# Layernorm's small arithmetic as a chain on GpSimd, and exponentials, masks and shift on two tiles at once, in a four-layer graph network

## The chip, the cores and the metric

The kernel runs on one core of a Trainium2 chip. The metric is the device time of one execution in microseconds, median of the runs. A profile comes from one further execution of the same program. Engines are called PE (TensorE, matrix products), DVE (VectorE), ACT (ScalarE), POOL (GpSimd) and SP (SyncE, which issues most DMAs here).

## The reference

32 batch elements, each with `x` of 512 nodes by 256 features and a 0/1 adjacency of 512 by 512, go through four attention layers. Every layer begins with the same step and ends with a residual sum:

```python
h = jnp.maximum(_layernorm(x, axis=-1), 0.0)   # (x - mean) / sqrt(var + 1e-5), then relu
x = x + layer(h, adj, ...)
```

- Layer 0: scores `(h att_W) h^T / sqrt(256)`, masked softmax, then twice `tanh(att (h W + b))`.
- Layer 1: scores `leaky_relu(src_i + dst_j)`, masked softmax, product with the values.
- Layer 2: `exp(-leaky_relu(s_i + d_j))` where there is an edge, divided by the row sum, then elu.
- Layer 3: scores with a bilinear term, leaky_relu, masked softmax, two more products, elu.

What the change touches is the mean and variance of layernorm in all four layers, and the exponential, mask and shift of the 512 by 512 scores in layers 1 to 3.

## The kernel before, in words

**Tiles.** 512 nodes are four tiles of 128 partitions. `x` of one batch element is a tile of 128 x 4 x 256 float32. The scores, transposed, are two tiles `e{l}_0` and `e{l}_1` of 128 x 2 x 512 float32 for each layer; `e(l, c)` is one 128 x 512 half of them. `codeT` holds the transposed adjacency in bfloat16.

**Who sets the order.** The program `graph(b, ...)` (L475) writes no instructions at once. Each `op(engine, cost, after, emit, tiles...)` notes a step: its engine, its cost as a pair of ns (how long it holds the engine, how long until its result can be used), the steps that it follows, and the tiles that it uses. `Plan.order` (L132) then plays all 32 elements with up to six in flight (`FLIGHT`, L244), gives each step a due time, and takes on each engine the ready step that is due first. `SLACK` (L68) stretches the costs for that: 1.03 for DVE (`V`) and ACT (`A`), 1.5 for POOL (`G`), and 0.8 us more for each DMA (`D`); 200 ns (`PASS`) go between steps. `Plan.best` (L91) tries several distances between the elements' due times and keeps the order that replays shortest. What comes out is one fixed order per engine, and each engine runs its list in that order; an instruction whose inputs are late holds up everything behind it on its engine.

**Layernorm**, `normed` (L552), in pairs of tiles, g = 0 and 1. For each tile `stats` (L556) runs `bn_stats` (L557, tile `st`: six numbers per row, among them the count-weighted statistics of the even and of the odd columns) and `bn_aggr` (L558, tile `mv`: mean and variance), both on DVE. For each pair DVE adds epsilon (`variance`, L561, tile `ve`), POOL takes the power -0.5 (`root`, L564, tile `rstd`), DVE forms minus mean times `rstd` (`offset`, L567, tile `off`). ACT then normalizes and clips each tile (`norm`, L571, tile `xn`). After it a copy splits `xn` into 16-bit planes (L576, on DVE, in layer 1 on ACT), SP issues a transposing DMA (L579, `planesT`), and ACT joins the planes to `hT` (L591), from which DVE makes sums `hs` (L664, L667) and PE the layer's products. Only in layer 0 of the first element are the tiles transposed by PE (L584).

**Scores of layers 1 and 2.** `leaky_exp_t` (L705) runs a leaky relu (L732) and an exponential (L735) for each of four tiles on ACT; `masked1` (L956) and `masked2` (L986) mask each tile on DVE. **Layer 3**: leaky relu (L1086, ACT), minus a row's maximum `crest` (L1089, DVE), exponential (L1092, ACT), each on four tiles. In every layer `attend` (L748) multiplies the tiles with the values on PE, tile by tile in the order c = 0 to 3 (L758).

**POOL** otherwise issues the weight loads at the start (L342) and the store of each finished element (L1154).

The pair of DVE's cost for `stats` and the costs of the power that the planner uses before the change:

```python
V_STATS, V_XN, V_TINY, V_TWO = (525.0, 610.0), (322.0, 407.0), (80.0, 165.0), (255.0, 340.0)
G_POW, G_STORE = (800.0, 850.0), (900.0, 900.0)
```

Of the kernel before, what the change touches and what calls it, by code (L numbers as in the profile page):

```python
# [11 lines left out]
F32 = mybir.dt.float32  # L12
# [3 lines left out]
AF = mybir.ActivationFunctionType  # L16
ALU = mybir.AluOpType
PSUM = bass.MemoryType.PSUM

P = 128  # L20
EPS = 1e-5
ALPHA = 0.2
NEG_INF = -(2.0**53)
TINY = 2.0**-100
# [11 lines left out]
    return t, t + 170.0  # L36


V_STATS, V_XN, V_TINY, V_TWO = (525.0, 610.0), (322.0, 407.0), (80.0, 165.0), (255.0, 340.0)
V_MASK, V_CODE, V_HALF, V_PSUM, V_ADD = (602.0, 683.0), (600.0, 690.0), (600.0, 690.0), (395.0, 484.0), (334.0, 425.0)  # L40
A_COPY, A_HALF, A_PRELU, A_EXP, A_TANH = (477.0, 597.0), (253.0, 373.0), (570.0, 693.0), (519.0, 640.0), (373.0, 474.0)
A_BIAS, A_PRELU2 = (570.0, 687.0), (629.0, 722.0)
G_POW, G_STORE = (800.0, 850.0), (900.0, 900.0)
V_SUM, V_BLOCK = (334.0, 425.0), (790.0, 880.0)
A_HALF_BIAS = (345.0, 460.0)
A_NORM, A_JOIN, V_SPLIT = (491.0, 590.0), (620.0, 767.0), (332.0, 422.0)
D_TURN = (1310.0, 2600.0)
# [159 lines left out]
def kernel(  # L207
# [48 lines left out]
    cols, pair, stat, turned = [P, HC, N], [P, NT, H], [P, NT], [P, NT, N]  # L256
# [8 lines left out]
        "code": (turned, BF16, "code"), "adj": (turned, I32, "adj"),  # L265
        "planes": ([P, 2, H], U16, "planes"), "planesT": ([P, 2 * HC, P], U16, "planesT"),
        "bank": ([P, 512], F32, "bank"), "v": (None, F32, "v"),
        "st": ([P, NT, 6], F32, None), "mv": ([P, NT, 2], F32, None), "sT": ([P, P], F32, "sT"),
        "ve": (stat, F32, None), "rstd": (stat, F32, None), "rs": (stat, F32, None), "off": (stat, F32, None),
# [155 lines left out]
    for n, dst, w, key in (("w0", w0_s, w0, "raw9"), ("att", att_s, att_w, "raw10")):  # L425
# [11 lines left out]
    a = [load(l1_sb, rows_of(l1_w), "raw0")]  # L437
    t = transposed(l1_sb, lambda: halves(l1_wide()), a, "raw0", "raw11")
# [36 lines left out]
    def graph(b, adj_before, x_before):  # L475


        T = Tiles(b)

        def op(engine, cost, after, emit, *keys, size=0, weights=()):  # L480
            return plan.op(engine, cost, after, emit, b, T.uses(keys) + W.uses(weights), size)

        def two(g):
            return slice(2 * g, 2 * g + 2)
# [67 lines left out]
        def normed(l, xs):  # L552
# [2 lines left out]

            def stats(t):  # L556
                nc.vector.bn_stats(T[f"st{l}"][:, t, :], T["x"][:, t, :])  # L557
                nc.vector.bn_aggr(T[f"mv{l}"][:, t, :], T[f"st{l}"][:, t, :])  # L558

            def variance(g):  # L560
                nc.vector.tensor_scalar(T[f"ve{l}"][:, two(g)], T[f"mv{l}"][:, two(g), 1], EPS, None, ALU.add)  # L561

            def root(g):
                nc.gpsimd.tensor_tensor(T[f"rstd{l}"][:, two(g)], T[f"ve{l}"][:, two(g)], mhalf[:, two(g)], ALU.pow)  # L564

            def offset(g):
                nc.vector.scalar_tensor_tensor(T[f"off{l}"][:, two(g)], T[f"mv{l}"][:, two(g), 0], -1.0,  # L567
                                               T[f"rstd{l}"][:, two(g)], ALU.mult, ALU.mult)

            def norm(t):  # L570
                nc.scalar.activation(T[f"xn{l}"][:, t, :], T["x"][:, t, :], AF.Relu,  # L571
# [23 lines left out]
            for g in range(NT // 2):  # L595
                a, d = (op("V", V_STATS, [xs[t]], partial(stats, t), "x", "slot") for t in (2 * g, 2 * g + 1))
                if b == l == 0:
                    for n in ("w0", "att"):
                        ready[n][0]["after"].append(d)
                a = op("V", V_TINY, [a, d], partial(variance, g))  # L600
                r = op("G", G_POW, [a], partial(root, g))
                r = op("V", V_TINY, [r], partial(offset, g))
                for t in (2 * g, 2 * g + 1):
                    flat, over = f"planes{l}_{t}", f"planesT{l}_{t}"
                    a = op("A", A_NORM, [r], partial(norm, t), "x", f"xn{l}")
                    if b == l == 0:
# [98 lines left out]
        def leaky_exp_t(l, vs, sign):  # L705
# [40 lines left out]
            return [op("A", A_EXP, [x], partial(exp, c), f"e{l}_{c // 2}") for c, x in enumerate(ls)]  # L746

        def attend(l, es, vs, use):  # L748

# [202 lines left out]
            xs += [op("V", V_MASK, [a], partial(add_z, g), "z0", "x")] * 2  # L952


        def masked1(c):
            nc.vector.scalar_tensor_tensor(e(1, c), T["codeT"][:, c, :], TINY, e(1, c), ALU.max, ALU.min)  # L956

        hs = normed(1, xs)
        right_after, right = block_sums("hs1", "hT1", lambda j, l: T["hT1"][:, j, half(l)], hs, left=False)
        vb = scored_values(1, right_after, right, l1_aug, ready["l1"])  # L960
        vs = [tuple(vb.values())] * NT
        es = leaky_exp_t(1, vs, 1.0)
        es = [op("V", V_MASK, [a], partial(masked1, c), "codeT", f"e1_{c // 2}") for c, a in enumerate(es)]
# [18 lines left out]
        vs = [tuple(vb.values())] * NT  # L982
        es = leaky_exp_t(2, vs, -1.0)

        def masked2(c):
            nc.vector.scalar_tensor_tensor(e(2, c), T["codeT"][:, c, :], 0.0, e(2, c), ALU.not_equal, ALU.mult)  # L986

        es = [op("V", V_MASK, [a], partial(masked2, c), "codeT", f"e2_{c // 2}") for c, a in enumerate(es)]

        def third(t, a, key):  # L990
            def sums():
# [87 lines left out]
        def shift():  # L1079
            return T["crest3"][:, 2:4, :].rearrange("p r n -> p (r n)").bitcast(F32)  # L1080
# [4 lines left out]
        def leaky3(c):  # L1085
            nc.scalar.activation(e(3, c), e(3, c), AF.Prelu, bias=zero, alpha=ALPHA)  # L1086

        def shifted(c):
            nc.vector.tensor_tensor(e(3, c), e(3, c), shift(), ALU.subtract)  # L1089

        def exp3(c):
            nc.scalar.activation(e(3, c), e(3, c), AF.Exp)  # L1092
# [108 lines left out]
```

## Time and profile before

| | before |
|---|---|
| median of 3 runs | 2353.38 us (2353.06 to 2353.42) |
| span of the profiled execution | 2353.1 us, 0.3 us under that median; no other time of that execution is given |
| PE busy | 2328.9 us |
| DVE busy | 2099.7 us |
| ACT busy | 1719.9 us |
| POOL busy | 254.2 us |
| granted TensorE clock, mean | 0.999 |
| DMA | 178.26 MB, mean 76 GB/s |

A line of the window view gives a stretch (us from the start of the span), its length, and then the busy us of PE, PEld (weight loads of PE), DVE, ACT and POOL with their numbers of instructions, the granted PE clock, the DMA engines' share and GB/s. A line of a group gives the line of the kernel, engine, operation, written and read tile, shapes and count, then total busy us, mean ns of one, and the idle time of the engine just before it with what ended it. A line of the timeline or the chain begins with the start and the length in us; neighbours that are alike are merged (`x2`). L12 is line 12 of the kernel before.

### The profile page before, as it was taken

How to read it: one execution, taken by the hardware profiler on the slowest of the kernel's cores; microseconds unless marked ns; L12 is line 12 of the kernel's file. 1: busy time of each engine (PE TensorE's matmuls, PEld its weight loads, DVE VectorE, ACT ScalarE, POOL GpSimd, SP SyncE). 2: the span in 40 equal slices, each digit the busy share in tenths (PEclk: the TensorE clock that was granted, in tenths of full speed). 3: DMA queues.
4: the chain of work that ended last, by engine and by line, in shares of the span. 5: the costliest groups of instructions: out<-in, count | busy, mean ns of one | idle time of the engine just before them, and what ended most of it. 6: DMA issues, size and time to landing. Idle time of an engine off the chain costs nothing.

```text
span 2353.1 us, 37623 instructions
## 1 busy us (share of the span) xinstructions
PE 2328.9 (99%) x12374; PEld 1992.0 (85%) x12374; DVE 2099.7 (89%) x6060; ACT 1719.9 (73%) x3421; POOL 254.2 (11%) x316
## 2 busy tenths in 40 slices
PE   8999999999999999999999999999999999999998
PEld 5789888888888888888898888888888888888887
DVE  8788899989889898898998889989898988987998
ACT  5677778767787677786777877677776778667874
POOL 3000101111011111011110010100101000010110
PEclk9999999999999999999999999999999999999999
DMA  7431233323333332333323334233343333321221
GB/s 192 106 78 28 57 79 79 88 66 83 72 75 84 78 83 66 70 88 90 82 58 74 80 85 90 54 82 70 88 91 68 86 68 73 86 54 33 55 49 42
DMA packets 429859, 178.26 MB, mean 76 GB/s; under 512 B 384128, under 2 KB 401664, under 8 KB 429664
## 3 DMA queue, kind: packets, MB, share of 16 engines
q1 hardware_dynamic: 424288, 157.51, 31.2%
q0 software_dynamic: 5232, 18.23, 2.4%
q8 instruction: 97, 1.59, 0.3%
q14 instruction: 98, 0.80, 0.1%
q10 hardware_dynamic: 144, 0.13, 0.0%
HBM read 67.64 MB, written 16.89 MB: 36 GB/s over the span
## 4 chain that ended last, share of the span: by engine, by line
PE 94%; DVE 4%; DMA 1%; ACT 1%; issue 0%; POOL 0%; DVEq 0%; ACTq 0%
PE bank_a L758 36%; PE bank_z L918 9%; PE bank_s3p L1040 5%; PE bank_o L936 4%; PE bank_q0p L874 4%; PE bank_f3p L783 4%; PE bank_w3p L809 4%; PE bank_v0p L809 4%; PE bank_f0p L783 4%; PE bank_s3q L1040 3%; PE bank_q0q L874 3%; PE bank_v1p L809 2%; PE bank_v3p L809 2%; PE bank_v2p L809 2%; PE bank_v3q L809 2%; PE bank_v1q L809 2%
## 5 line engine op out<-in xcount | busy, mean ns | idle before, releaser
L758 PE MATMUL bank_a<-v,e 128*128 128x258 f32 (+2 forms) x4096 | 1017.7, 381 | 0.9 <-DVE e L956 0.9
L758 PEld LDWEIGHTS bank_a<-v,e 128*128 128x128 f32 x4096 | 744.1, 190 | 108.9 <-issue 18.2
L591 ACT COPY hT<-planesT 128x512 uint16<-128x512 uint16 x508 | 377.8, 769 | 93.9 <-DMA planesT<-planes 93.2
L564 POOL TENSOR_TENSOR rstd<-ve,mhalf 128x2 f32<-128x2 f32 x256 | 216.0, 863 | 1732.3 <-DVE ve L561 1599.4
L571 ACT ACTIVATE xn<-x,off,rstd 128x256 f32<-128x256 f32 x512 | 278.0, 593 | 39.8 <-DVE off L567 38.9
L918 PE MATMUL bank_z<-e,y 128*128 128x512 f32 x512 | 240.8, 593 | 0.0
L557 DVE BATCH_NORM_STATS2 st<-x 128x6 f32<-128x256 f32 x512 | 210.5, 411 | 3.8 <-DMA x<-in_x_dram 3.8
L576 DVE COPY planes<-xn 128x512 uint16<-128x512 uint16 x380 | 156.4, 420 | 17.3 <-DMA planesT<-planes 10.2
L882 ACT ACTIVATE e<-e 128x512 f32<-128x512 f32 x124 | 77.8, 629 | 121.9 <-DVE e L893 61.8
L732 ACT ACTIVATE e<-row,v 128x512 f32<-128x512 f32 x224 | 156.6, 719 | 0.8 <-DMA row<-row 0.7
L735 ACT ACTIVATE e<-e 128x512 f32<-128x512 f32 x256 | 157.1, 630 | 0.0
L918 PEld LDWEIGHTS bank_z<-e,y 128*128 128x128 f32 x512 | 92.7, 190 | 64.9 <-issue 60.5
L695 ACT COPY v<-bank_v1p 128x258 f32<-128x258 f32 x128 | 47.7, 373 | 120.0 <-PE bank_v1p L809 119.3
L936 PE MATMUL bank_o<-w_sb,zT 128*128 128x256 f32 x512 | 118.5, 379 | 0.2 <-ACT zT L922 0.2
L1047 DVE SCALAR_TENSOR_TENSOR e<-bank_s3p,v,mask 128x256 f32<-128x256 f32 x256 | 111.0, 475 | 8.4 <-PE bank_a L758 4.4
L558 DVE BATCH_NORM_AGGREGATE mv<-st 128x2 f32<-128x6 f32 x512 | 93.2, 182 | 17.5
L936 PEld LDWEIGHTS bank_o<-w_sb,zT 128*128 128x128 f32 x512 | 95.8, 190 | 12.8 <-ACT zT L922 0.6
L664 DVE TENSOR_TENSOR hs<-hT,hs 128x256 f32<-128x256 f32 x254 | 105.1, 414 | 1.1
L667 DVE TENSOR_TENSOR hs<-hT 128x512 f32<-128x512 f32 x127 | 86.6, 682 | 14.5 <-ACT hT L591 14.3
L1086 ACT ACTIVATE e<-e,zero 128x512 f32<-128x512 f32 x128 | 88.2, 721 | 12.9 <-DVE crest L1064 11.4
L885 DVE TENSOR_TENSOR e<-bank_q0p,mask 128x512 f32<-128x512 f32 x124 | 84.5, 682 | 13.8 <-PE bank_q0p L874 12.3
L1089 DVE TENSOR_TENSOR e<-e,crest 128x512 f32<-128x512 f32 x128 | 85.9, 682 | 8.3 <-ACT crest L1083 8.1
(202 smaller groups left out, 4891.3 us busy)
## 6 DMA issues: line engine op xcount, KB each, us to landing
adj<-in_adj_dram SPq DMA_DIRECT2D x128, 256.0 KB
x<-in_x_dram SPq DMA_DIRECT2D x31, 512.0 KB
out_dram<-y POOLq DMA_DIRECT2D x31, 512.0 KB, 3.6
row<-row SPq DMA_DIRECT2D x56, 256.0 KB
planesT<-planes SPq DMA_TRANSPOSE x508
codeT<-code SPq DMA_TRANSPOSE x124
crest<-crest SPq DMA_TRANSPOSE x64
row<-sT SPq DMA_DIRECT2D x56, 2.0 KB
```

The costliest lines, as they stand in the source:

```text
L557: nc.vector.bn_stats(T[f"st{l}"][:, t, :], T["x"][:, t, :])
L564: nc.gpsimd.tensor_tensor(T[f"rstd{l}"][:, two(g)], T[f"ve{l}"][:, two(g)], mhalf[:, two(g)], ALU.pow)
L571: nc.scalar.activation(T[f"xn{l}"][:, t, :], T["x"][:, t, :], AF.Relu, bias=T[f"off{l}"][:, t : t + 1], scale=T[f"rstd{l}"][:, t : t + 1])
L591: nc.scalar.copy(bits[:, :, :, t * P : (t + 1) * P], T[f"planesT{l}_{t}"].rearrange("p (b c) n -> p b c n", b=2))
L735: nc.scalar.activation(e(l, c), e(l, c), AF.Exp, scale=sign)
L758: nc.tensor.matmul(T[key][:, : LEAD + H + 1 - lead], e(l, c)[:, t * P : (t + 1) * P], T[f"v{l}"][:, c, lead:], start=(c == 0), stop=(c == ...
L783: nc.tensor.matmul(p[:, : N // 2], w[:, x - 1, :], right(x), start=fresh, stop=True, skip_group_check=True)
L809: nc.tensor.matmul(p[:, j * k : (j + 1) * k], right(x)[:, j * P : (j + 1) * P], w[:, x - 1, :], start=fresh and j == 0, stop=True, skip_gr ...
L874: nc.tensor.matmul(p[:, j * N // 2 : (j + 1) * N // 2], right(x)[:, j * P : (j + 1) * P], left(x), start=fresh and j == 0, stop=True, skip ...
L918: nc.tensor.matmul(T[f"bank_z{k}"], T["y0"][:, c, k * P : (k + 1) * P], e(0, c), start=(c == 0), stop=(c == NT - 1))
L936: nc.tensor.matmul(T[key][:, j * H : (j + 1) * H], T["zT"][:, k, t * P : (t + 1) * P], w1_sb[:, k, :], start=(k == 0), stop=(k == HC - 1))
L1040: nc.tensor.matmul(p[:, j * N // 2 : (j + 1) * N // 2], left(x)[:, j * P : (j + 1) * P], right(x), start=fresh and j == 0, stop=True, skip ...
```

## The change

On DVE `stats` keeps only `bn_stats`. Aggregation, variance, power and offset of a pair of tiles become `moments`: ten instructions on POOL on 128 x 2 numbers, one step of the plan. They compute the variance from the two halves' statistics as (sum of both) / 256 + eps + (difference of the means)^2 / 4, and the offset as minus half the sum of the means times `rstd`. In layers 1 to 3 the exponential, in layers 1 and 2 the mask, and in layer 3 the leaky relu and the shift too take a whole `e{l}_{g}` of 128 x 2 x 512 in one instruction; the leaky relu of layers 1 and 2 stays by tile, and the attention's products follow the pair's step in place of the tile's. The planner's costs change with them.

```diff
-V_STATS, V_XN, V_TINY, V_TWO = (525.0, 610.0), ...
+V_STATS, V_XN, V_TINY, V_TWO = (340.0, 425.0), ...
-G_POW, G_STORE = (800.0, 850.0), (900.0, 900.0)
+G_CHAIN, G_STORE = (2200.0, 2250.0), (900.0, 900.0)
+V_SUM, V_BLOCK, V_FULL = (334.0, 425.0), (790.0, 880.0), (1140.0, 1225.0)
+A_EXP_TWO, A_PRELU_TWO = (960.0, 1070.0), (1050.0, 1160.0)
...
             def stats(t):
                 nc.vector.bn_stats(T[f"st{l}"][:, t, :], T["x"][:, t, :])
-                nc.vector.bn_aggr(T[f"mv{l}"][:, t, :], T[f"st{l}"][:, t, :])
-
-            def variance(g):
-                nc.vector.tensor_scalar(ve, mv[..., 1], EPS, None, ALU.add)
-            def root(g):
-                nc.gpsimd.tensor_tensor(rstd, ve, mhalf[:, two(g)], ALU.pow)
-            def offset(g):
-                nc.vector.scalar_tensor_tensor(off, mv[..., 0], -1.0, rstd, ALU.mult, ALU.mult)
+            def moments(g):
+                st = T[f"st{l}"][:, two(g), :]
+                gap, total, var, rstd, off = (T[f"{n}{l}"][:, two(g)] for n in ("gap", "sum", "var", "rstd", "off"))
+                gp = nc.gpsimd
+                gp.tensor_tensor(gap, st[:, :, 1], st[:, :, 4], ALU.subtract)
+                gp.tensor_tensor(var, st[:, :, 2], st[:, :, 5], ALU.add)
+                gp.tensor_tensor(gap, gap, gap, ALU.mult)
+                gp.tensor_scalar(var, var, 1.0 / H, EPS, ALU.mult, ALU.add)
+                gp.tensor_scalar(gap, gap, 0.25, None, ALU.mult)
+                gp.tensor_tensor(var, var, gap, ALU.add)
+                gp.tensor_tensor(rstd, var, mhalf[:, two(g)], ALU.pow)
+                gp.tensor_tensor(total, st[:, :, 1], st[:, :, 4], ALU.add)
+                gp.tensor_scalar(total, total, -0.5, None, ALU.mult)
+                gp.tensor_tensor(off, total, rstd, ALU.mult)
...
-                a = op("V", V_TINY, [a, d], partial(variance, g))
-                r = op("G", G_POW, [a], partial(root, g))
-                r = op("V", V_TINY, [r], partial(offset, g))
+                r = op("G", G_CHAIN, [a, d], partial(moments, g))
...
-            def exp(c):
-                nc.scalar.activation(e(l, c), e(l, c), AF.Exp, scale=sign)
+            def exp(g):
+                nc.scalar.activation(T[f"e{l}_{g}"], T[f"e{l}_{g}"], AF.Exp, scale=sign)
...
-        def masked1(c):
-            nc.vector.scalar_tensor_tensor(e(1, c), T["codeT"][:, c, :], TINY, e(1, c), ALU.max, ALU.min)
+        def masked1(g):
+            nc.vector.scalar_tensor_tensor(T[f"e1_{g}"], T["codeT"][:, two(g), :], TINY, T[f"e1_{g}"], ALU.max, ALU.min)
...
-        def shifted(c):
-            nc.vector.tensor_tensor(e(3, c), e(3, c), shift(), ALU.subtract)
+        def shifted(g):
+            nc.vector.tensor_tensor(T[f"e3_{g}"], T[f"e3_{g}"], shift().unsqueeze(1).to_broadcast([P, 2, N]), ALU.subtract)
...
```

`masked2`, `leaky3` and `exp3` are changed in the same way as these three.

More of the change, by code (lines that the diff above doesn't have):

```diff
@@ L36, in pe @@
     return t, t + 170.0
-V_STATS, V_XN, V_TINY, V_TWO = (525.0, 610.0), (322.0, 407.0), (80.0, 165.0), (255.0, 340.0)
+V_STATS, V_XN, V_TINY, V_TWO = (340.0, 425.0), (322.0, 407.0), (80.0, 165.0), (255.0, 340.0)
 V_MASK, V_CODE, V_HALF, V_PSUM, V_ADD = (602.0, 683.0), (600.0, 690.0), (600.0, 690.0), (395.0, 484.0), (334.0, 425.0)
@@ L42 @@
 A_BIAS, A_PRELU2 = (570.0, 687.0), (629.0, 722.0)
-G_POW, G_STORE = (800.0, 850.0), (900.0, 900.0)
-V_SUM, V_BLOCK = (334.0, 425.0), (790.0, 880.0)
+G_CHAIN, G_STORE = (2200.0, 2250.0), (900.0, 900.0)
+V_SUM, V_BLOCK, V_FULL = (334.0, 425.0), (790.0, 880.0), (1140.0, 1225.0)
+A_EXP_TWO, A_PRELU_TWO = (960.0, 1070.0), (1050.0, 1160.0)
 A_HALF_BIAS = (345.0, 460.0)
@@ L267 @@
         "bank": ([P, 512], F32, "bank"), "v": (None, F32, "v"),
-        "st": ([P, NT, 6], F32, None), "mv": ([P, NT, 2], F32, None), "sT": ([P, P], F32, "sT"),
-        "ve": (stat, F32, None), "rstd": (stat, F32, None), "rs": (stat, F32, None), "off": (stat, F32, None),
+        "st": ([P, NT, 6], F32, None), "sT": ([P, P], F32, "sT"),
+        "gap": (stat, F32, None), "sum": (stat, F32, None), "var": (stat, F32, None),
+        "rstd": (stat, F32, None), "rs": (stat, F32, None), "off": (stat, F32, None),
         "top": (stat, BF16, None),
@@ L557, in stats @@
                 nc.vector.bn_stats(T[f"st{l}"][:, t, :], T["x"][:, t, :])
-                nc.vector.bn_aggr(T[f"mv{l}"][:, t, :], T[f"st{l}"][:, t, :])
-            def variance(g):
-                nc.vector.tensor_scalar(T[f"ve{l}"][:, two(g)], T[f"mv{l}"][:, two(g), 1], EPS, None, ALU.add)
-            def root(g):
-                nc.gpsimd.tensor_tensor(T[f"rstd{l}"][:, two(g)], T[f"ve{l}"][:, two(g)], mhalf[:, two(g)], ALU.pow)
-            def offset(g):
-                nc.vector.scalar_tensor_tensor(T[f"off{l}"][:, two(g)], T[f"mv{l}"][:, two(g), 0], -1.0,
-                                               T[f"rstd{l}"][:, two(g)], ALU.mult, ALU.mult)
+            def moments(g):
[12 more added lines that the diff above has]
+                gp.tensor_tensor(off, total, rstd, ALU.mult)
             def norm(t):
@@ L745, in leaky_exp_t @@
             ls = [op("A", A_PRELU if turned else A_PRELU2, [a], partial(leaky, c), key, v, f"e{l}_{c // 2}") for c in range(NT)]
-            return [op("A", A_EXP, [x], partial(exp, c), f"e{l}_{c // 2}") for c, x in enumerate(ls)]
+            return [op("A", A_EXP_TWO, ls[two(g)], partial(exp, g), f"e{l}_{g}") for g in range(NT // 2)]
         def attend(l, es, vs, use):
@@ L962, in graph @@
         es = leaky_exp_t(1, vs, 1.0)
-        es = [op("V", V_MASK, [a], partial(masked1, c), "codeT", f"e1_{c // 2}") for c, a in enumerate(es)]
+        es = [op("V", V_FULL, [es[g]], partial(masked1, g), "codeT", f"e1_{g}") for g in (0, 1)]
+        es = [es[c // 2] for c in range(NT)]
         def second(t, a, key):
@@ L983, in graph, with masked2 @@
         es = leaky_exp_t(2, vs, -1.0)
-        def masked2(c):
-            nc.vector.scalar_tensor_tensor(e(2, c), T["codeT"][:, c, :], 0.0, e(2, c), ALU.not_equal, ALU.mult)
-        es = [op("V", V_MASK, [a], partial(masked2, c), "codeT", f"e2_{c // 2}") for c, a in enumerate(es)]
+        def masked2(g):
+            nc.vector.scalar_tensor_tensor(T[f"e2_{g}"], T["codeT"][:, two(g), :], 0.0, T[f"e2_{g}"], ALU.not_equal, ALU.mult)
+        es = [op("V", V_FULL, [es[g]], partial(masked2, g), "codeT", f"e2_{g}") for g in (0, 1)]
+        es = [es[c // 2] for c in range(NT)]
         def third(t, a, key):
@@ L1083, in leaky_row, with leaky3, exp3 @@
             nc.scalar.activation(shift(), T["crest3"][:, 0, :], AF.Prelu, bias=zero, alpha=ALPHA)
-        def leaky3(c):
-            nc.scalar.activation(e(3, c), e(3, c), AF.Prelu, bias=zero, alpha=ALPHA)
-        def shifted(c):
-            nc.vector.tensor_tensor(e(3, c), e(3, c), shift(), ALU.subtract)
-        def exp3(c):
-            nc.scalar.activation(e(3, c), e(3, c), AF.Exp)
+        def leaky3(g):
+            nc.scalar.activation(T[f"e3_{g}"], T[f"e3_{g}"], AF.Prelu, bias=zero, alpha=ALPHA)
+        def shifted(g):
+            nc.vector.tensor_tensor(T[f"e3_{g}"], T[f"e3_{g}"], shift().unsqueeze(1).to_broadcast([P, 2, N]), ALU.subtract)
+        def exp3(g):
+            nc.scalar.activation(T[f"e3_{g}"], T[f"e3_{g}"], AF.Exp)
         hi = [op("V", V_MASK, [ls[2 * g]], partial(higher, g), f"e3_{g}", "crest3") for g in range(2)]
@@ L1099, in graph @@
         row = op("A", A_PRELU2, [a], leaky_row, "crest3")
-        ls = [op("A", A_PRELU2, [a, hi[c // 2]], partial(leaky3, c), f"e3_{c // 2}") for c, a in enumerate(ls)]
-        ls = [op("V", V_MASK, [a, row], partial(shifted, c), "crest3", f"e3_{c // 2}") for c, a in enumerate(ls)]
-        es = [op("A", A_EXP, [a], partial(exp3, c), f"e3_{c // 2}") for c, a in enumerate(ls)]
+        ls = [op("A", A_PRELU_TWO, [ls[2 * g], hi[g]], partial(leaky3, g), f"e3_{g}") for g in (0, 1)]
+        ls = [op("V", V_FULL, [ls[g], row], partial(shifted, g), "crest3", f"e3_{g}") for g in (0, 1)]
+        es = [op("A", A_EXP_TWO, [ls[g]], partial(exp3, g), f"e3_{g}") for g in (0, 1)]
+        es = [es[c // 2] for c in range(NT)]
         def block_w(i, l):
```

## The prediction

> **What bounds the kernel now.** I read the page, then the busy time in windows, the chain that ended last, the groups of each engine, and timelines. TensorE (PE) is busy for all but 24.2 us of the span:
>
> ```profile
> span 2353.1 us, 37623 instructions
> ...
> PE 2328.9 (99%) x12374; PEld 1992.0 (85%) x12374; DVE 2099.7 (89%) x6060; ACT 1719.9 (73%) x3421; POOL 254.2 (11%) x316
> ```
>
> Nothing in this diff lowers PE's 2328.9 us, since no matmul is touched. In the chain that ended last the same `bank_o` stretch returns after 71.94 us, one batch element:
>
> ```profile
> 890.72 3.45 PE bank_o L936 x16
> ...
> 962.66 3.45 PE bank_o L936 x16
> ```
>
> In the window view (the stretch, its length, then busy us of PE, PEld, DVE, ACT, POOL) PE has no idle time in the middle; the loss is at the two ends:
>
> ```profile
> 0.00:40.00 40.00, 31.17 (x122) 20.80 (x123) 31.61 (x123) 20.52 (x39) 18.67 (x40) 1.00 0.84 221
> 40.00:80.00 40.00, 38.54 (x207) 31.85 (x206) 36.00 (x109) 23.61 (x46) 2.68 (x4) 1.00 0.55 119
> ...
> 1000.00:1040.00 40.00, 40.00 (x208) 33.15 (x207) 36.65 (x106) 31.30 (x63) 5.07 (x6) 1.00 0.45 102
> ...
> 2240.00:2280.00 40.00, 36.06 (x180) 30.81 (x179) 37.60 (x116) 34.96 (x74) 5.07 (x6) 0.96 0.20 43
> ```
>
> Of the 24.2 us, 8.8 lie before the first matmul, 1.5 between 40 and 80, some 6.5 behind the last matmul, and nearly all of the remaining 7.4 after 1880 (3.9 from 2240 to 2280). From 80 to 2120 PE is busy for 2038.4 of 2040 us. So the change can earn hardly more than the 9 us of waits inside the run; it can lose without such a limit, because every engine runs a fixed order.
>
> **What goes.** From DVE: 512 aggregations (L558, 93.2 us busy, 182 ns each), 256 variances (L561, 37.6 us), 256 offsets (L567, 37.3 us), 168 us in all. And six pairs of 128x512 operations per element (L956, L986, L1089) become 128x1024. One takes 683 ns, a 128x256 `hs` (L664) 414: 256 columns cost 269, 1024 columns 683 + 2 x 269 = 1221, so a pair saves 145 and 192 pairs 28 us. DVE falls from 2100 to some 1904 us. On ACT the exponentials (L735 630 ns, L1092 632) and L1086 (721) are joined: by L999 (469 for 256 columns, beside 630 for 512) a join saves 308 ns, 256 joins 79 us at most. Between 80 and 2120 all this lies beside a PE that never waits: **nothing is earned there**. What covers it is PE's 71.94 us per element; DVE needs 65.6 of them now.
>
> **What comes: a chain of ten on POOL, 256 times.** Today POOL does only the power. The trace has no small POOL arithmetic; its nearest rows (busy us, mean ns):
>
> ```profile
> L564 POOL TENSOR_TENSOR rstd<-ve,mhalf 128x2 f32<-128x2 f32 x256 | 216.0, 863 | 1732.3 <-DVE ve L561 1599.4 <-DVE off L567 53.6 <-ACT xn L571 25.8
> ...
> masks.py:199 POOL TENSOR_SCALAR_AFFINE_SELECT ident<-ident 128x128 f32<-128x128 f32 x1 | 0.3, 284 | 0.0
> ...
> masks.py:197 POOL MEMSET ident<- 128x128 f32 x1 | 0.2, 204 | 0.3 <-POOLq L1187 0.3
> ...
> L326 POOL MEMSET minus<- 128x1 f32 x1 | 0.1, 95 | 0.0
> ```
>
> The two memsets give 0.86 ns a column, so the select at 2 columns would take 284 - 126 x 0.86 = 176 ns. I take that for each of the nine (bounds: 95, the memset, and 863, the power), and 0.08 us for the hand-over to a dependent one (from `ve`'s end to the power's start in the timeline), six times: 9 x 0.176 + 6 x 0.08 + 0.69 (the power undisturbed) = 2.75 us. POOL also waits for DVE. The view of L564 gives the power's spread, and the timeline shows a slow pair:
>
> ```profile
> L564 POOL TENSOR_TENSOR rstd<-ve,mhalf x256: 678/706/2346, 7.2 to 2279.2; 128x2 f32<-128x2 f32 x128
> ```
>
> ```profile
> 506.14 0.68 DVE L1009 SCALAR_TENSOR_TENSOR x<-y,x 128x512 f32<-128x512 f32 x1
> 506.24 2.33 POOL L564 TENSOR_TENSOR rstd<-ve,mhalf 128x2 f32<-128x2 f32 x2 [9.16 <-DVE ve L561]
> 506.74 0.68 DVE L519 TENSOR_SCALAR code<-adj 128x1024 bf16<-128x1024 int32 x1
> ```
>
> Two powers take 2.33 us beside these DVE operations, 1.38 in the quiet head. The mean is 863 - 690 = 173 ns over the undisturbed power; ten such waits are 1.7. **One chain: 4.4 us** (bounds: 9 x 0.095 + 0.69 = 1.5, and ten powers, 8.6).
>
> The Trainium skill ("SBUF — State Buffer", Who interferes with whom) says that a DVE instruction with two SBUF inputs and a GpSimd instruction that reads SBUF exclude each other, whoever starts second waiting for the other's whole instruction. The slow pair agrees with it; the mean row shows that a wait is usually much shorter than a whole DVE operation. By the strict form, ten full waits of 0.68 us, the chain would be an estimated 2.75 + 6.8 = 9.6 us; by the row it is 4.4.
>
> What does the chain replace? Not the 0.69 us of a power: `ve` and `off` stand in DVE's queue. At 613.69 two `ve` start, the powers end at 615.27, and the `off` run at 615.98 and 616.73, behind masks and sums. Over all 256 in the trace (k-th `ve` to k-th `off`) it is 2.9 us in the median and 3.4 in the mean from the start of the one to the end of the other, and the aggregation adds 0.2 ahead. So `xn` comes some 0.8 us later. In the 68 cases of 256 where two powers are asked for within 2 us, the second chain queues behind the first and its `xn` comes about 5 us later.
>
> The order knows of it: it is built with 2.25 x 1.5 = 3.4 us per chain, so my chain is 1.0 us late on it, a second one 2.0. Behind `xn` on ACT stand the evacuations of PE's banks. What takes up the delay is ACT's idle 27% and the 0.8 us that the order adds to each DMA, one of which (the transposition) follows every `xn`. Cost in the middle: from 0 to the rival's price; I take 1.6 us, a doubling of the 1.6 us that slip there now. On POOL itself stores and weight loads queue behind the chain; a store only frees its slot, 40 us before anyone asks (POOL idles 42.5 us ahead of one).
>
> **Head.** Tiles 0 and 1 have their statistics at about 5.4 us when no aggregation stands between. With DVE nearly idle the chain is 2.75 us: 8.2, as now (8.1). The second chain ends at 10.9, where `off` ended at 9.3: 1.6 us later, less what PE can multiply of `bank_v` meanwhile. I take +1.0 (0 to 1.6; weight loads behind more chains could add the 1.5 us again that PE waits between 40 and 80).
>
> **Tail.** From 2250 to 2272 PE idles 3.3 us and DVE is busy 20.8 of 22. There DVE loses 7 aggregations, 4 `ve`, 4 `off` and four joins: 1.3 + 0.6 + 0.6 + 0.6 = 3.1 us. Against it stands the later `xn`, 0.8 to 5 us, in the layers that nothing else covers. I take -1.5 (from -3.3 to +4).
>
> **Sum:** 1.6 + 1.0 - 1.5 = +1.1 us on the span of 2353.1, 2354.2; the median of the runs stands 0.3 above that span: **2354.5 us**. Ends without a rival: 2353.4 - 3.3 (tail) - 3.5 (the other waits after 1880) = 2346.6, and 2353.4 + 1.6 (middle) + 3.1 (head and loads) + 4 (tail) = 2362.1.
>
> **Rivals.** *Within a few us* (the sum above): 2354.5, 2349 to 2358.
>
> *POOL becomes late, slower.* Place: `xn` at the head of ACT's queue. DVE operations that read two SBUF tensors follow one another (414 to 683 ns, after the join 1221), so a chain of dependent reads may meet one each time: with half a 0.55 us operation per step, 2.75 + 10 x 0.27 = 5.4 us, 2.0 late on the order, 1.2 after the DMA's 0.8. If one chain in 25 passes that to PE (a guess; ACT idles for 27%), 10 x 1.2 = 12 us: **2366**. It decides from a chain of 4.2 us up (3.4 + 0.8); at 71.94 / 8 = 9.0 us POOL itself would be the bound. For it: mean over median in the power's row. Against: the old path through DVE was nearly as long.
>
> *DVE's relief fills the tail, faster.* If the chain is 3.4 us or less, `xn` comes no later than now, and of the 7.4 us of waits near the end and the 1.5 in the head some 7 go: **2346**. For it: DVE at 20.8 of 22 us where PE waits. Against: ACT is at 20.5 of 22 there too.
>
> *It does not relieve DVE*, since POOL's reads hold DVE up: DVE has 6 us per element to spare, so this too is within a few us, without the tail's gain: 2356.
>
> **Chances.** About 0.2% (4.7 us) is what a measurement of this kernel can tell from no change: under 2348.7 is faster, over 2358.1 slower. Within a few us, with the last rival: 0.44; POOL late: 0.36; tail filled: 0.20. The range takes in the faster rival and most of the slower one: 2346 to 2370.
>
> **What would show it.** The first POOL step takes about 176 ns and a chain about 4.4 us from first start to `off`; DVE falls to some 1904 us, ACT to 1640 to 1700; the period stays at 71.94; PE idles nearer 10 than 8.8 us at the start. It is wrong if the period grows, if ACT shows long waits for POOL ahead of `xn`, or if PE's waits after 1880 vanish or double.

## The result, and the profile after

| | before | after |
|---|---|---|
| median of 4 runs each | 2353.22 us (2352.96 to 2353.42) | 2364.28 us (2363.70 to 2365.25) |
| ratio to before | | 1.0046 (95% interval 1.0032 to 1.0060) |
| span of the profiled execution | 2353.1 us | 2363.0 us |

The change costs 11.1 us, where 1.1 were forecast. That is inside the range, and on the side and near the price of the rival "POOL becomes late" (2366); the likeliest case, 2349 to 2358, did not come. A later profiled execution of the kernel before, where span and time are both given, took 2352.58 us with a span of 2350.8: 1.8 us lie around the span, as after the change (2364.85 and 2363.0). The profiled execution of before was so some 1.5 us slower than its usual run, and the two profiles differ by 9.9 us.

The head of the page after (span, then busy us, share and instructions of each engine):

```profile
span 2363.0 us, 38600 instructions
...
PE 2331.4 (99%) x12374; PEld 1989.5 (84%) x12374; DVE 1980.0 (84%) x4844; ACT 1702.3 (72%) x3165; POOL 851.2 (36%) x2620
```

DVE lost 120 us and ACT 18; POOL gained 597. PE idles 31.6 us in place of 24.2. The window view after, with the columns of the prediction's:

```profile
0.00:20.00 20.00, 8.79 (x26) 5.71 (x27) 11.95 (x39) 5.42 (x10) 12.15 (x57) 1.00 0.77 243
20.00:40.00 20.00, 19.04 (x80) 12.44 (x79) 13.68 (x36) 11.94 (x23) 17.97 (x46) 1.00 0.70 161
...
80.00:2120.00 2040.00, 2036.25 (x10804) 1740.77 (x10803) 1718.75 (x4201) 1490.83 (x2776) 732.75 (x2262) 1.00 0.33 76
2120.00:2200.00 80.00, 80.00 (x439) 68.78 (x437) 58.91 (x139) 56.49 (x107) 19.25 (x66) 1.00 0.17 39
2200.00:2363.00 163.00, 148.94 (x834) 129.95 (x832) 144.03 (x345) 112.47 (x203) 46.28 (x124) 0.99 0.21 47
```

The number of matmuls has to be read beside the busy time. The same stretch of the middle before:

```profile
80.00:2120.00 2040.00, 2038.36 (x10835) 1747.69 (x10835) 1825.59 (x5259) 1507.13 (x3003) 212.27 (x250) 1.00 0.34 76
```

It has 10835 matmuls, and after the change 10804; at 2040 / 10835 = 0.188 us each, 31 fewer are 5.8 us. PE's busy time shows only 2.1 us of it. A matmul's record outlasts the start of the next one (379 ns for 256 columns in `bank_o`, where the next starts after 216), so a start that is up to 0.16 us late leaves no gap, and the late matmul itself is recorded some 0.1 us longer. So the loss is counted from start to start here: for every matmul the time to the next one's start, less the undisturbed pace of its shape. The choice of that pace shifts the middle of all kernels together by up to 1 us, so the differences between kernels count, and a value near 0 means no loss.

| us lost by PE | before the first matmul | 0-80 | 80-300 | 300-2120 | 2120-2200 | 2200-end | span |
|---|---|---|---|---|---|---|---|
| before | 8.8 | 5.5 | -0.1 | 1.9 | 2.5 | 8.8 | 2353.1 |
| after | 10.5 | 6.9 | 0.5 | 7.8 | -0.1 | 12.2 | 2363.0 |

After less before: 3.1 us up to 80, 0.6 and 5.9 in the middle, -2.6 and +3.4 near the end, -0.6 behind the last matmul, together 9.9 with rounding. There are two questions: the start, and the middle.

**The start**, in the timeline after:

```profile
6.85 0.20 POOL L565 TENSOR_TENSOR gap<-st 128x2 f32<-128x2 f32 x1 [5.30 <-DVE st L559]
...
8.29 0.72 POOL L571 TENSOR_TENSOR rstd<-var,mhalf 128x2 f32<-128x2 f32 x1
...
9.56 0.20 POOL L574 TENSOR_TENSOR off<-sum,rstd 128x2 f32<-128x2 f32 x1
...
9.80 1.09 ACT L577 ACTIVATE xn<-x,off,rstd 128x256 f32<-128x256 f32 x2 [7.14 <-POOL off L574]
...
10.45 1.18 PE L590 MATMUL bank_n<-ident,xn 128*128 128x128 f32 x4 [10.45 <-ACT xn L577]
```

An undisturbed chain takes 6.85 to 9.76, 2.9 us, and PE waits for it. Statistics begin 0.7 us later than before (5.35, were 4.64), since `x` landed later in this execution. The second chain ends at 12.92 and the weight loads on POOL begin at 18.7, where it was 12.6.

**The middle**, in the chain that ended last: the share by engine on the page, then stretches from its list.

```profile
PE 81%; POOL 7%; DVE 5%; ACT 4%; issue 2%; DMA 1%; POOLq 0%; SPq 0%; ACTq 0%; DVEq 0%
```

```profile
977.60 1.73 PE bank_o L940 x8
...
1024.29 0.48 POOL off L574
...
1029.37 1.04 POOL off L574
...
1030.94 0.58 ACT xn L577
1031.52 0.26 ACT v L699
...
1034.67 0.27 ACT v L699
...
1034.98 1.57 PE bank_a L762 x6
...
1050.02 1.73 PE bank_o L940 x8
```

Before, PE had 94% and POOL 0% of this chain. Now it runs through two POOL chains back to back, then on ACT through `xn` and the copies `v` out of PE's banks, to PE; and the same `bank_o` stretch returns after 72.42 us in place of 71.94. (Single elements take 69 to 78 us, so the loss is read from the table and not from one period.) The longest wait of PE that the view names between 300 and 2120 is 0.7 us. That looks like the slower rival. The experiments say how far it is.

### The profile page after: what moved, and what is told of

Same layout as the page of the kernel before. It is cut to its first block, busy times and chain, and to the rows that moved or that the text cites. A ratio compares the mean times of both kernels' runs of the same rounds, so it can differ in the third digit from the quotient of the medians.

```text
span 2363.0 us, 38600 instructions
## 1 busy us (share of the span) xinstructions
PE 2331.4 (99%) x12374; PEld 1989.5 (84%) x12374; DVE 1980.0 (84%) x4844; ACT 1702.3 (72%) x3165; POOL 851.2 (36%) x2620
## 4 chain that ended last, share of the span: by engine, by line
PE 81%; POOL 7%; DVE 5%; ACT 4%; issue 2%; DMA 1%; POOLq 0%; SPq 0%; ACTq 0%; DVEq 0%
PE bank_a L762 30%; PE bank_z L922 9%; PE bank_o L940 5%; PE bank_s3p L1046 4%; PE bank_q0p L878 4%; PE bank_f3p L787 4%; PE bank_f0p L787 4%; PE bank_v0p L813 3%; PE bank_w3p L813 3%; PE bank_s3q L1046 3%; PE bank_q0q L878 2%; PE bank_v3p L813 2%; POOL rstd L571 2%; PE bank_v1p L813 2%; PE bank_v2p L813 2%
## 5 line engine op out<-in xcount | busy, mean ns | idle before, releaser
L762 PE MATMUL bank_a<-v,e 128*128 128x258 f32 (+2 forms) x4096 | 1040.3, 381 | 5.7 <-ACT v L699 1.5
L565 POOL TENSOR_TENSOR gap<-st 128x2 f32<-128x2 f32 x256 | 77.5, 303 | 792.1 <-DVE st L559 737.2
L1161 POOL DMA_DIRECT2D out_dram<-y x31 | 25.8, 831 | 584.3 <-DVE y L1144 551.8
L571 POOL TENSOR_TENSOR rstd<-var,mhalf 128x2 f32<-128x2 f32 x256 | 209.2, 817 | 20.1
L559 DVE BATCH_NORM_STATS2 st<-x 128x6 f32<-128x256 f32 x512 | 191.4, 415 | 6.0 <-DMA x<-in_x_dram 5.6
L699 ACT COPY v<-bank_v3p 128x258 f32<-128x258 f32 x128 | 48.0, 375 | 128.8 <-PE bank_v3p L813 128.8
L739 ACT ACTIVATE e<-e 128x1024 f32<-128x1024 f32 x128 | 135.9, 1062 | 0.9
L960 DVE SCALAR_TENSOR_TENSOR e<-codeT,e 128x1024 f32<-128x1024 bf16 x64 | 78.3, 1223 | 38.5 <-ACT e L739 37.2
L703 DVE TENSOR_TENSOR v<-v,bank_v2q 128x258 f32<-128x258 f32 x96 | 40.4, 421 | 77.8 <-PE bank_v2q L813 73.4
L886 ACT ACTIVATE e<-e 128x512 f32<-128x512 f32 x124 | 78.9, 640 | 25.0 <-DVE e L897 23.3
```

Of the source, the lines that this page charges most:

```text
L571: gp.tensor_tensor(rstd, var, mhalf[:, two(g)], ALU.pow)
L762: nc.tensor.matmul(T[key][:, : LEAD + H + 1 - lead], e(l, c)[:, t * P : (t + 1) * P], T[f"v{l}"][:, c, lead:], start=(c == 0), stop=(c == ...
```

## The experiments

The expectations speak of theories by letters. In short, A: the chain's length on POOL reaches PE through `xn`. B: the two-tile steps hand their results on later. C: neither matters, the planner found a less lucky order. D: it is DVE's two-tile steps together with the chain. A ratio stands against the kernel before, run on the same chip (2353.2 to 2354.1 us). "Before" and "after" name the kernels before and after the change.

### The parts alone

The chain alone, with exponentials, masks and shift by tile as before:

```diff
-            def exp(g):
-                nc.scalar.activation(T[f"e{l}_{g}"], T[f"e{l}_{g}"], AF.Exp, scale=sign)
+            def exp(c):
+                nc.scalar.activation(e(l, c), e(l, c), AF.Exp, scale=sign)
...
```

`masked1`, `masked2`, `leaky3`, `shifted` and `exp3` go back in the same way.

> The chain of ten on GpSimd alone, with its planner costs; exponentials, masks and shift by tile as before. Theory A (the chain makes the normalized tile late, at the start and a little in every element): most of the 11 us of the whole change is here, 2360 to 2364 us, first matmul near 10.4 us, small PE waits in every element. Theory B (the joined two-tile steps make the attention start later): 2354 to 2356 us, only the start is late. Theory C (neither costs anything by itself, the new order is just a worse one): any value, no relation to the other runs.

Measured: 2360.02 us, 1.0031 (1.0019 to 1.0042). The size is as theory A had it, the place is not: from 300 to 2120 this kernel loses 0.5 us, less than before (1.9), with a period of 71.94 us in most elements. Its loss is at the start, in 80 to 300 (4.9 us) and near the end (11.2).

The two-tile steps alone, with the old layernorm:

```diff
-                r = op("G", G_CHAIN, [a, d], partial(moments, g))
+                a = op("V", V_TINY, [a, d], partial(variance, g))
+                r = op("G", G_POW, [a], partial(root, g))
+                r = op("V", V_TINY, [r], partial(offset, g))
```

> The two-tile exponentials, masks and shift alone; layernorm on DVE with the power on GpSimd as before. Theory A: 2350 to 2354 us, since only DVE and ACT are relieved, period 71.94 us per element, first matmul at 8.8 us. Theory B: 2358 to 2362 us with waits in every element. Theory C: any value.

Measured: 2357.03 us, 1.0015 (1.0007 to 1.0024), between the two expectations. It earns nothing and loses a little, again not in the middle (1.4 us there).

### The planner's cost

The kernel before, with nothing changed but what the planner believes of the power:

```diff
-G_POW, G_STORE = (800.0, 850.0), (900.0, 900.0)
+G_POW, G_STORE = (2200.0, 2250.0), (900.0, 900.0)
```

> The kernel before, instruction for instruction, but planned as if the power on GpSimd took 2.2 us (the cost of the chain), so that only the order differs. Theory A: the order plans the normalized tile 2 us later than it comes, which costs a little at the start, 2353 to 2356 us, and no waits in the middle. Theory C (the order is what costs): 2360 us or more.

Measured: 2355.56 us, 1.0009 (1.0000 to 1.0018). The first matmul starts at 11.5 us in this order, and the time hardly moves.

The kernel after, with the planner told the measured chain:

```diff
-G_CHAIN, G_STORE = (2200.0, 2250.0), (900.0, 900.0)
+G_CHAIN, G_STORE = (3000.0, 3700.0), (900.0, 900.0)
```

> The changed kernel, planned with the chain's measured length (3.0 us on the engine, 3.7 to its result) in place of 2.2. Theory A in the form that the order is taken by surprise: the waits in the middle go, 2357 to 2360 us, the late start stays. Theory A in the form that the delay costs by itself: 2363 to 2366 us, as the change. Theory B: no difference from the change, 2364 us.

Measured: 2363.70 us, 1.0043 (1.0030 to 1.0057): nothing gained. Yet POOL is off the path: 0% of the chain, and the wait view (us in total, times, longest) has almost no ACT waiting for it. Its lines from 300 to 2120:

```profile
ACT xn L577 <- POOL off L574: 11.7, 2, 8.2
...
PEld bank_z L922 <- DVE v L703: 5.3, 22, 0.2
...
PEld bank_v2p L813 <- ACT v L699: 4.6, 22, 0.2
```

Here two hand-offs of 0.2 us repeat in 22 elements, 5.3 + 4.6 = 9.9 us of waits on PE's weight loads, and PE's loss by starts in this stretch is 7.3. All but two of 24 elements take 72.32 to 72.34 us, 0.39 over 71.94. **The same loss as after, with another last step**: an evacuation of `v`, and no POOL before it.

### The order kept

The kernel before with its order as it stands; only what the steps issue differs. Aggregation, variance and offset issue nothing, and the ten instructions stand in the power's place:

```diff
-                nc.gpsimd.tensor_tensor(T[f"rstd{l}"][:, two(g)], T[f"ve{l}"][:, two(g)], mhalf[:, two(g)], ALU.pow)
+                moments(g)
```

> The order of the kernel before is kept step for step; only, the ten GpSimd instructions run where the power ran, and the aggregation, variance and offset are left out of DVE's list. Nothing else is joined. Theory A (the chain's length is what costs): the order expects a result after 0.85 us and gets it after 3.5, so ACT waits ahead of the normalized tile and PE behind it in every element: 2365 to 2385 us. Theory C (the new order costs, not the chain): 2352 to 2355 us.

Measured: 2374.60 us, 1.0091 (1.0076 to 1.0107), 20.5 us over before. The theory that only the order differs falls. The chain that ended last has POOL in it, by its shares:

```profile
PE 85%; POOL 6%; DVE 4%; ACT 3%; issue 1%; DMA 1%; SPq 0%; DVEq 0%; POOLq 0%; ACTq 0%
```

It loses 10.2 us from 300 to 2120, 8.2 more than before. The delay from a pair's statistics to `off` is not longer in the median: 3.9 us, where before it was 4.8. It has a floor (none is under 2.97, where 47 of before's were), but the floor is not what PE meets. The order is the same, so each matmul can be set beside its counterpart before. In the middle PE falls further behind eight times, by 0.85 to 2.1 us, and each time the chain of waits leads back over `xn` to a pair that had not been hurried before (3.2 to 5.2 us, here 5.9 to 9.2), and whose chain had queued behind another. Five of the eight are alike, one in every fourth element. The first of them, from the timelines of POOL, ACT and PE:

```profile
549.20 0.20 POOL L573 TENSOR_TENSOR off<-sum,rstd 128x2 f32<-128x2 f32 x1
549.35 0.20 POOL L564 TENSOR_TENSOR gap<-st 128x2 f32<-128x2 f32 x1
...
553.27 0.20 POOL L573 TENSOR_TENSOR off<-sum,rstd 128x2 f32<-128x2 f32 x1
...
553.50 0.60 ACT L585 ACTIVATE xn<-x,off,rstd 128x256 f32<-128x256 f32 x1 [0.78 <-POOL off L573]
554.00 0.46 ACT L807 ACTIVATE fa<-bank_f3p,l_u 128x256 f32<-128x256 f32 x1
...
554.51 0.70 PE L797 MATMUL bank_f3p<-hs,m 128*128 128x256 f32 x2 [0.17 <-ACT fa L807]
```

The same second `off` and the same matmuls before, from the timelines of DVE and PE:

```profile
545.29 0.15 DVE L567 SCALAR_TENSOR_TENSOR off<-mv,rstd 128x2 f32<-128x2 f32 x1
...
547.38 0.60 PE L783 MATMUL bank_f3p<-hs,m 128*128 128x256 f32 x2
```

There the second `off` ended 5.24 us after the pair's statistics, here 7.07. Before, it stood 1.9 us ahead of the matmuls; here they wait for it. Of the 18.4 us between the two profiles 6.8 come up to 300 us, 8.2 in the middle and 3.4 behind it.

Ten more dependent instructions on POOL, which add zero to `off`:

```diff
+                spare = gap
+                gp.tensor_tensor(spare, total, rstd, ALU.mult)
+                for i in range(7):
+                    gp.tensor_tensor(spare, spare, rstd, ALU.mult)
+                gp.tensor_tensor(spare, spare, spare, ALU.subtract)
+                gp.tensor_tensor(off, off, spare, ALU.add)
```

> The changed kernel with ten more dependent small instructions behind each chain, which add zero; the planner is told nothing of them. Theory A: a chain of 6.5 to 7.5 us in place of 3.7, ACT waits for GpSimd grow from 160 us to 500 or more, PE waits in every element, 2385 to 2420 us. Theory C: 2364 us.

Measured: 3042.30 us, 1.2925 (1.2907 to 1.2942), far over the 2385 to 2420 of theory A. The mean chain grew from 3.7 to 6.5 us, and the time by 678 us. Lines of its page (busy, and the chain's share) and of its waits:

```profile
PE 2545.8 (84%) x12374; PEld 2107.3 (69%) x12374; DVE 1990.2 (65%) x4844; ACT 1697.8 (56%) x3165; POOL 1375.4 (45%) x5180
...
POOL 43%; PE 32%; issue 10%; DVE 9%; ACT 5%; DMA 0%; POOLq 0%; ACTq 0%; SPq 0%; DVEq 0%
```

```profile
ACT xn L583 <- POOL off L580: 865.3, 243, 9.1
```

POOL is busy for 45% only: it is latency that costs, not POOL's throughput. A second chain waits for the first, and from statistics to `off` the median is 12.7 us. PE's busy time rose by 214 us although its matmuls are the same, for the granted clock fell to 0.924 in the mean. What the last 2.8 us of a chain cost is out of all proportion to the first 2.9.

### The start

The kernel after, with layer 0 of the first six elements on the old path through DVE:

```diff
+            early = l == 0 and b < FLIGHT
...
-                r = op("G", G_CHAIN, [a, d], partial(moments, g))
+                if early:
+                    a = op("V", V_TINY, [a, d], partial(variance, g))
+                    r = op("G", G_POW, [a], partial(root, g))
+                    r = op("V", V_TINY, [r], partial(offset, g))
+                else:
+                    r = op("G", G_CHAIN, [a, d], partial(moments, g))
```

> The changed kernel, but layer 0 of the first six elements has its aggregation, variance and offset on DVE and only the power on GpSimd, as before. If the start of the changed kernel (first 80 us, 3.1 us of the 9.9 between the two profiles) is the chain's doing, the first matmul is back near 8.8 us and the time falls by 2 to 4 us, to 2360 to 2362; if the late start is only swallowed further on, 2364.

Measured: 2361.45 us, 1.0031 (1.0019 to 1.0043), 2.8 under after in the medians. Its first window:

```profile
0.00:20.00 20.00, 10.90 (x37) 7.24 (x38) 13.09 (x54) 6.89 (x12) 7.38 (x24) 1.00 0.96 288
```

PE has 37 matmuls there, after had 26; the first starts at 8.6 us. The middle loses 7.7 as in after. So the start is the chain's price, about 3 us in this kernel, and is apart from the middle.

### Which join

The chain with ACT's steps joined and DVE's by tile (the cut shows the difference from the chain alone; `leaky3` and `exp3` likewise):

```diff
-            def exp(c):
-                nc.scalar.activation(e(l, c), e(l, c), AF.Exp, scale=sign)
+            def exp(g):
+                nc.scalar.activation(T[f"e{l}_{g}"], T[f"e{l}_{g}"], AF.Exp, scale=sign)
```

> The changed kernel with ACT's exponentials and layer 3's leaky relu joined, but DVE's masks and shift by tile as before. Theory A' (the 1.22 us DVE instructions hold the chain up, which makes the waits of the middle): GpSimd's small steps fall back to the means of the chain alone, waits in the middle go, 2359 to 2361 us. Theory B (the joins delay attention): half of the middle's waits stay, 2361 to 2363.

Measured: 2352.72 us, 0.9996 (0.9988 to 1.0005), the time of before and under both expectations. The middle loses nothing:

```profile
80.00:2120.00 2040.00, 2039.92 (x10849) 1749.41 (x10848) 1743.57 (x4385) 1489.87 (x2787) 721.19 (x2266) 1.00 0.34 76
```

14 more matmuls than before, 45 more than after. In the mean the chains are no shorter (3.64 us, after 3.70), so it is not the typical chain that DVE's joined operations make dear. The share of chains that follow another back to back fell, from 157 of 255 in after to 85. That alone does not decide either: it is 80 to 103 in the chain alone, in the kept order, with DVE's steps joined and in the two kernels with the planner's corrected cost, and two of these five have the loss. The two together are counted below.

The chain with DVE's steps joined and ACT's by tile:

```diff
-            def masked1(c):
-                nc.vector.scalar_tensor_tensor(e(1, c), T["codeT"][:, c, :], TINY, e(1, c), ALU.max, ALU.min)
+            def masked1(g):
+                nc.vector.scalar_tensor_tensor(T[f"e1_{g}"], T["codeT"][:, two(g), :], TINY, T[f"e1_{g}"], ALU.max, ALU.min)
...
```

`masked2` and `shifted` are joined in the same way.

> The changed kernel with DVE's masks and shift joined and the chain on GpSimd, but ACT's steps by tile: the corner that is missing. Theory D (the chain and DVE's joined steps do not go together): waits in the middle of 5 us or more, 2362 to 2368 us. If ACT's join has a part in it: 2357 to 2360 and no waits in the middle.

Measured: 2356.50 us, 1.0013 (1.0004 to 1.0021). The theory that the chain and DVE's two-tile steps are enough to make the loss falls: the middle loses -0.5 us, that is, nothing. And in this kernel the waits of ACT for POOL are longer in total than in any other but the doubled chain. The waits of the kernel with ACT joined, then those of this one:

```profile
ACT xn L577 <- POOL off L574: 184.6, 100, 6.1
```

```profile
ACT xn L577 <- POOL off L574: 280.1, 118, 5.8
```

In after they are 160.0 us in 139 times. 280 us of waits came with no loss in the middle, and the 24 us (in the whole span) of the planner's corrected cost with 7 us: **a wait on ACT ahead of `xn` is no sign of a loss**; only whether PE is reached counts.

ACT's steps joined, without the chain:

```diff
-            return [op("A", A_EXP, [x], partial(exp, c), f"e{l}_{c // 2}") for c, x in enumerate(ls)]
+            return [op("A", A_EXP_TWO, ls[two(g)], partial(exp, g), f"e{l}_{g}") for g in range(NT // 2)]
```

> ACT's exponentials and layer 3's leaky relu joined, nothing else: layernorm with the power on GpSimd, masks and shift by tile, as before. If ACT's join is a gain of its own (it made the chain's 2360.0 into 2352.7), 2346 to 2350 us. If it only made up for what the chain costs, 2352 to 2355.

Measured: 2360.84 us (2357.91 to 2364.15), 1.0033 (1.0021 to 1.0046): both expectations wrong. With no chain at all the profiled execution, the slowest of the five, loses 12.5 us from 300 to 2120, the most of any but the doubled chain, and the longest wait of PE there is another hand-off again (us in total, times, longest):

```profile
PE bank_f3p L784 <- ACT fa L794: 4.2, 5, 1.7
```

### The best version

The chain with ACT's steps joined, and layer 0 of the first six elements on the old path, as in the run on the start:

```diff
+            early = l == 0 and b < FLIGHT
...
+                    r = op("V", V_TINY, [r], partial(offset, g))
```

> Chain on GpSimd and ACT's steps joined, DVE's by tile (2352.7 us before), and layer 0 of the first six elements on DVE as before. If the start's loss is the chain's there too (first matmul at 9.4, 4.4 us of waits in the first 20), 2349 to 2351 us, faster than both kernels; if another order swallows it, 2352 to 2354.

Measured: 2351.29 us, 0.9991 (0.9982 to 1.0000), 1.4 under the same without the old start, and the lowest of all. It is 2 us under before, less than the 0.2% that can be told from no change.

The same kernel with ACT joined, with the planner's cost corrected:

```diff
-G_CHAIN, G_STORE = (2200.0, 2250.0), (900.0, 900.0)
+G_CHAIN, G_STORE = (3000.0, 3700.0), (900.0, 900.0)
```

> Chain on GpSimd and ACT's steps joined, DVE's by tile, but planned with the chain's measured length (3.0 us on the engine, 3.7 to its result): the same instructions in another order. If 2352.7 us is the work's and not one order's luck, 2351 to 2355 us; Theory C (orders differ by luck): 2356 to 2362.

Measured: 2353.98 us, 1.0001 (0.9992 to 1.0010). Three pairs of kernels differ by the planner's cost alone; measured against before, they lie 2.0, 0.9 and 2.1 us apart. The 11 us of the change are more than that.

### What is shown, and what stays open

| steps | us against before | PE's loss 300-2120 |
|---|---|---|
| chain | +6.5 | 0.5 |
| ACT joined | +7.6 | 12.5 |
| ACT and DVE joined | +3.5 | 1.4 |
| chain, ACT joined | -1.4 (other cost +0.7) | -0.6 (-0.6) |
| chain, DVE joined | +3.3 | -0.5 |
| chain, ACT and DVE joined (the change) | +11.1 (other cost +10.1) | 7.8 (7.3) |

(The numbers in brackets are of the same instructions, planned with the corrected cost.)

*What reaches PE in after.* Between 300 and 2120 us 47 matmuls start over 50 ns late, 9.1 us in all. Followed back in the trace, 42 of them, with 7.9 us, lead over ACT (`v` or `w`, then `xn`) to 23 of the 201 chains there. All 23 are long, 4.8 to 5.7 us where the mean is 3.7: in each, one or two steps of 0.2 us last 0.8 to 1.3 us beside a joined shift or mask of DVE. And 21 of them had first waited 1.6 to 2.6 us for the chain ahead. The stretch at 1029.37 shown above is one of these. So PE meets the two delays almost only where they fall together. Counted from 300 to 2120, chains that followed another within 0.3 us and then took over 4.5 us:

| kernel | such chains | PE's loss 300-2120 |
|---|---|---|
| the change | 25 | 7.8 |
| the change, old start | 25 | 7.7 |
| chain alone | 1 | 0.5 |
| chain, ACT joined (and with the other cost) | 0 (0) | -0.6 (-0.6) |
| chain, DVE joined | 0 | -0.5 |
| the change, other cost | 1 | 7.3 |
| kept order | 2 | 10.2 |

The last two lose without them, and by other ways: the one at hand-offs that no chain stands behind, the other by chains that queued in an order made for a power of 0.85 us.

*Shown:* the start's 3 us are the chain's (2.8 come back with the old start, 1.4 where ACT's steps are joined). At a fixed order the chain costs 20 us; the planner's new order brings the chain alone to 6.5, and with ACT's steps joined to nothing. The parts do not add: the two dearest parts, chain and ACT's join, are together free. The loss in the middle of the change comes by second chains that a joined operation of DVE stretches. At which hand-off PE loses differs from kernel to kernel (`v` with POOL and `xn` ahead of it, `v` alone, `fa`). With the planner's corrected cost it is two hand-offs that miss by 0.2 us in nearly every element.

*Open:* why the planner finds a tight order for the full change, twice, and a loose one when DVE's or ACT's steps stay by tile. Nor is it shown that the change would lose nothing if its second chains were kept apart from the joined shifts: the one new order that did so lost as much elsewhere. DVE's join alone was not run, and the change was not run in an order taken from another kernel. After less before also has +3.4 us from 2200 to the end, which no experiment took apart; the others, but the doubled chain, range there from 8.2 to 12.0.

## Why the prediction was right or wrong

**Nothing is earned: right.** DVE's and ACT's relief lay beside a full PE. The sizes were off: DVE fell to 1980, not 1904, since busy time counts overlapping records once: the durations of DVE's records add up to 191 us less (196 worked out), the busy time falls by 120. A joined exponential takes 1062 ns, saving 2 x 630 - 1062 = 198, not 308: the row taken for its slope (L999) reads other operands. ACT stands at 1702, just above the 1640 to 1700. DVE's joined steps take 1216 to 1223 ns, worked out as 1221.

**The chain's length: right in size, a little high.** 0.19 to 0.22 us for a small step (0.176 taken), 2.9 undisturbed (2.75), 3.7 in the mean beside DVE (4.4). Waits on DVE are 0.8 us a chain, not 1.7. The lock that the prediction cites from the Trainium skill ("SBUF — State Buffer", Who interferes with whom) is right in kind where it bites, in the timeline of after:

```profile
1026.54 1.37 POOL L571 TENSOR_TENSOR rstd<-var,mhalf 128x2 f32<-128x2 f32 x1
...
1027.99 2.36 DVE L1095 TENSOR_TENSOR e<-e,crest 128x1024 f32<-128x1024 f32 x2
1028.01 1.27 POOL L573 TENSOR_SCALAR sum<-sum 128x2 f32<-128x2 f32 x1
...
1029.37 1.03 POOL L574 TENSOR_TENSOR off<-sum,rstd 128x2 f32<-128x2 f32 x1
```

Two small steps wait out two joined shifts of 1.2 us each. As an average, ten full waits (9.6 us) are refuted by the 3.7.

**The middle: 1.6 us taken, 6.5 came** (0.6 up to 300, 5.9 behind it). This is the step that failed. The term was sized by a typical chain, 4.4 us long and 0.8 later than the old path, and put at a doubling of what slipped before. The mean chain is even shorter, 3.7 us, and yet PE loses, because the loss comes from the few chains that both queued and were stretched. The prediction had each half: "the second chain queues behind the first", and DVE's joined operations of 1221 ns that a chain of reads may meet. It gave the first no price of its own, and it carried the 68 cases of 256 over from the old order; in the new one 157 chains of 255 follow another back to back. From statistics to `off` the mean went from 5.1 to 6.2 us, and to 6.9 to 8.3 for the 21 that reach PE.

**"It decides from a chain of 4.2 us up": half right.** The 23 chains that reach PE in after are all longer than that. But the rule was laid on all chains alike, with 5.4 us and "one chain in 25" at 1.2 us each. Here it was one in nine, with 0.1 to 0.6 us each: nearly three times as many, at less than a third of the price. And length alone is not sufficient: the kernel with ACT joined has nine chains over 4.5 us in the middle, none of them queued, and loses nothing.

**The head: 1.0 taken, 3.1 came.** 1.7 is the first matmul (0.7 of it the later `x`), the rest the second chain and what follows. The weight loads did move, 6 us later on POOL; the window from 40 to 80 lost 2.1 us, before 3.0, but the one from 20 to 40 lost 1.3, before 0.1. The bound given, 3.1, held.

**The tail: -1.5 taken, +0.2 came** (-2.6, +3.4, -0.6). DVE's relief filled one wait and another opened.

**The rivals.** The slower one had the right side, place and nearly the price, 2366; it had a chance of 0.36 against 0.44 for the case that did not come. That its price was nearly met is luck in good part: it came out of a guess, 12 us in the middle, and what came was 6.5 there and 3 at the start, which it had not counted. That the range held rests on the same guess, since its upper end was set to take in this rival. The sign named for it, waits of ACT for POOL, was there (160 us), but kernels with more of them lose nothing. "DVE's relief fills the tail" did not come here; the kernel with ACT joined and the old start reaches 2351.3, not 2346.

**Profile and runs.** The median was taken as 0.3 us above the span, as its page had it; for one and the same execution it is 1.8. That moved the forecast by nothing that matters.

## What to carry to other kernels

When one engine is full and the others run fixed orders, ask of a moved step not only its mean delay but what happens when two are asked for together: the second waits for the first, and what stretches it then comes on top. With the order kept, the median delay fell from 4.8 to 3.9 us and the kernel lost 20 us; what PE lost in its middle came by second chains. A wait on a side engine, however long, is no loss until the full engine's own starts show it; count those, look for tenths of a microsecond that repeat from element to element, and follow each back to what held it up. And where a planner makes a new order for every edit, parts that lose alone can be free together and the reverse, so measure the combination, and vary the planner's cost to see how much is the order.

## What the runs showed of the hardware

The granted clock of PE fell when PE starved, in the kernel with the doubled chain. From its window view:

```profile
1000.00:1040.00 40.00, 29.61 (x146) 25.04 (x145) 25.19 (x65) 20.85 (x41) 23.85 (x99) 0.83 0.30 60
...
1016.00:1026.00 10.00, 5.51 (x16) 4.24 (x16) 3.83 (x8) 3.01 (x5) 8.00 (x33) 0.50 0.28 66
1033.00:1049.00 16.00, 13.65 (x91) 12.29 (x90) 13.37 (x31) 7.95 (x17) 10.38 (x34) 1.00 0.31 80
```

PE is busy for 29.6 of 40 us in the first stretch, at a clock of 0.83; in all, 0.924, and 214 us more busy time for the same matmuls. So the waits were paid a second time, as slower matmuls. The other two stretches show that the clock is either halved or full: in this trace it is 0.5 for 466 of 3026 us and otherwise 1.0, and it keeps a value for 3.41 us or multiples of that. The Trainium skill ("TensorE: Matmul & The Clock Gate", What's actually happening) has the clock halve after an idle window of about 3.4 us; the run agrees, in the halving and in the length of the pieces; the waits of PE's weight loads reach 9.6 us here.

Undisturbed, POOL's arithmetic on 128 x 2 numbers takes 0.19 to 0.22 us an instruction and starts every 0.15 us when the next one does not depend on it, every 0.27 to 0.30 when it does; the power is 0.72. From the first chain of after:

```profile
6.85 0.20 POOL L565 TENSOR_TENSOR gap<-st 128x2 f32<-128x2 f32 x1 [5.30 <-DVE st L559]
7.00 0.20 POOL L566 TENSOR_TENSOR var<-st 128x2 f32<-128x2 f32 x1
7.16 0.19 POOL L567 TENSOR_TENSOR gap<-gap 128x2 f32<-128x2 f32 x1
7.44 0.19 POOL L568 TENSOR_SCALAR var<-var 128x2 f32<-128x2 f32 x1
7.71 0.22 POOL L569 TENSOR_SCALAR gap<-gap 128x2 f32<-128x2 f32 x1
```
